# Inverse norms of the local attention heads: logarithm and exponential as seed, one Newton step, clamp on GpSimd

## Chip, cores, metric

The kernel runs on one core of one Trainium2 chip, in one launch, with float32 inputs and outputs. The metric is the device time of one execution in microseconds (us); the time before is the median of three runs. Engines are named as in the profile: PE (TensorE, with PEld for its weight loads), DVE (VectorE), ACT (ScalarE), POOL (GpSimd), SP (the DMA queue of SyncE). L12 is line 12 of the kernel before.

## What is computed

Four residual layers work on x (4 sequences of 512 tokens, 128 features). The change touches the third layer's second half alone, a local transformer of six blocks (reference cut to that):

```python
def attn_layer(x, Wqkv, qs, ksc, Wo):              # 16 heads of 64
    q, k, v = split_heads(x @ Wqkv)
    q = l2norm(q) * qs                             # t / max(norm(t), 1e-12)
    k = l2norm(k) * ksc
    q = q * cos * scale + rotate_half(q) * sin * scale
    k = k * cos * inv + rotate_half(k) * sin * inv
    out = local_attention(q, k, v)                 # windows of 32, each sees itself and the one before
    return out @ Wo
for i in range(6):
    x = attn_layer(shift_tokens(x), Wqkv[i], q_scale[i], k_scale[i], Wo[i]) + x
    x = ffn_layer(shift_tokens(x), ...) + x        # layer norm, gated gelu of width 341
```

The rotation doesn't change which factor a head is divided by, so the kernel rotates first and multiplies by the inverse norm afterwards.

## The kernel before

**Stages.** A preparation and a first part (two cross attentions, mixture of experts), a middle part, the local transformer (`local_transformer`, L1695), and a last part (cross attention, experts). The first, middle and last part are ordered by a small planner (`Plan`) with costs per engine. The local transformer isn't: it runs under a manual schedule, so that each engine executes its instructions in the order in which the loop from L2033 writes them.

**Tiles and pipeline.** The transformer has 96 tiles: 6 blocks, 4 sequences, 4 tiles of 128 tokens. Iteration n of the loop works on three tiles at once: T (number n) is projected and rotated, T1 (n - 1) gets its scores and softmax, T2 (n - 2) its average over the values and its output projection. Between them a feed-forward row F (one sequence of one block) advances by a quarter: `ff_stage` with phase 0 to 3 over four iterations. Four iterations are called a round below.

**The steps of a tile**, with the lines that the prediction uses:
- `queries_or_keys`: a product of y with 512 columns of the weights into a bank ps_mm (L1779, PE), and its square (L1781, ACT). Four of these per tile: q and k, two groups of eight heads each.
- `rotate`: on DVE the product with the cosine table (L1789), with the swapped sine table (L1792), and the sum of the squares per head (L1801, into ss); on POOL the sum of the two products (L1802).
- `normalise`, after the fourth rotation: clamp and scale of ss to -ss/2 (L1812, DVE), a bit-trick seed of 1/sqrt(ss) (L1813, DVE), three Newton steps of four operations each (L1817 to L1820, POOL), all on 128x32; then four products of the rotated heads with the inverse norms (L1823, POOL, 128x512).
- `turned`, an iteration later: transposes of the heads on PE (L582, helper `to_features`), copies to qT and kT on ACT (L1835), and for kT a copy of 32 columns of the tile before on POOL (L1831).
- `scores` on PE (L1879 the mask, L1888 the products) into the bank pair ps_sc; `softmax`: maximum and difference on DVE (L1898, L1899), exponential on ACT (L1904).
- `probabilities`: transposes of P on PE (L582) and copies on ACT (L1909); `average` on PE (L1919); `normalised` on DVE (L1928, L1929); `attended` copies on ACT (L1938); `project_out` on PE (L1943); `residual` on DVE (L1950).
- `values`: two products on PE (L1858), copied by ACT (L1859), then shifted by DMAs from SP.
- The feed-forward row: `ff_gate` (L1978, gelu L1981 on ACT), `ff_up` (L1989), `ff_down` (L2001), its layer norm with DVE's L522. These use ps_sc as well.

Transposes, value products and so on share two PSUM banks (ps_tr), and ps_sc is one pair of banks, so a reader that is late holds the next PE group back.

At the end of an iteration the order is: `rotate(T, 1, 1)`, `normalise(T)`, `softmax(T1)`, `project_out(T2)`, `residual(T2)`, `values(T)`. On DVE, L1812 and L1813 thus stand between the last rotation and the maximum L1898. On ACT, between the aT copies L1938 and the exponential L1904 there is nothing, in some iterations the copy of `swap` and a table load. In five iterations (the last of each block but the final one) `tables` puts six products on POOL ahead of the rotations' sums (L1760, L1766).

ACT's function tables are loaded where an instruction needs another set: in each feed-forward row once ahead of the gelu in phase 1 and once ahead of the first exponential after the gelu of phase 2.

Of the kernel before, what the change touches and what calls it, by code (L numbers as in the profile page):

```python
# [22 lines left out]
I32 = mybir.dt.int32  # L23
U32 = mybir.dt.uint32
AF = mybir.ActivationFunctionType
ALU = mybir.AluOpType
# [12 lines left out]
MASKED = -1e30  # L39
CAP0 = max(1, math.ceil(math.ceil(NTT * 128 * 2 * 1.25) / E))  # L40
CAP3 = int(round(2 * NTT * 128 * 1.05 / E))
NOWHERE = 1e6
ROW = D + 2
CH_W = [128, 128, DI - 256]
# [77 lines left out]
def bc(ap, shape, *axes):  # L122

    for a in axes:
        ap = ap.unsqueeze(a)
    return ap.to_broadcast(shape)
# [112 lines left out]
def tile_kernel(ctx: ExitStack, tc: tile.TileContext, A: dict, out: bass.AP):  # L239
    nc = tc.nc  # L240
    V, G, SC, PE, DMA = nc.vector, nc.gpsimd, nc.scalar, nc.tensor, nc.sync
# [21 lines left out]
    @contextmanager  # L263
    def planned():

        plan = Plan(engines, new_bank)
        yield plan
        with banks(), tc.manual_schedule():
            plan.run()
# [15 lines left out]
    def p_tr(*shape):  # L285
        return psum(shape, "tr", 2)
# [54 lines left out]
    for b in range(B):  # L341
        t = xpool.tile([128, NT, D], F32, name=f"x{b}", tag=f"x{b}")
# [26 lines left out]
    with banks(), tc.tile_pool(name="prep", bufs=1) as prep:  # L369
# [26 lines left out]
        t = p_tr(128, B, SK)  # L396
# [3 lines left out]
        t = p_tr(128, 4, D)  # L400
# [3 lines left out]
        t = p_tr(128, 8)  # L404
# [3 lines left out]
        t = p_tr(128, 2, E)  # L408
# [59 lines left out]
    def col(r):  # L468
        return cols[:, r : r + 1]
# [6 lines left out]
    sent, back = [], []  # L476
    for i, cap in enumerate((CAP0, CAP3, CAP3)):
        n = -(-E * cap // 128)
# [4 lines left out]
    def clear(pool, i):  # L483
# [5 lines left out]
        def fill(e):  # L489
            e.memset(t, 0.0)  # L490
            e.memset(t[:, 1, D + 1 :], NOWHERE)

# [362 lines left out]
    class Routing:  # L855
# [27 lines left out]
        def row(self, plan, b, after):  # L883
# [88 lines left out]
            def places(e):  # L972
                t = bank.view(128, nk, NT, E)
                for k in range(2):
                    j = k if self.apart else 0
                    if j == k:
                        c = rp.tile(full, F32, name="pl")
                        e.tensor_tensor(c, t[:, j], bc(self.limit[:, j], full, 1), ALU.is_ge)
                        e.scalar_tensor_tensor(
                            c, c, NOWHERE, t[:, j], ALU.mult, ALU.subtract if j else ALU.add  # L980
                        )
# [645 lines left out]
    def last_part():  # L1627

        with ExitStack() as es:
# [4 lines left out]
            b2 = yp.tile([128, E, D], BF16, name="b2")  # L1634
            R = Routing(mp, wr[:, 1], CAP3, True)
            with tc.tile_pool(name="xw3", bufs=2) as wp, planned() as plan:
# [18 lines left out]
            with tc.tile_pool(name="m3w", bufs=2) as wp, planned() as plan:  # L1655
# [21 lines left out]
                def down(e, e0, t, h):  # L1677
# [5 lines left out]
                sends, issued = experts(  # L1683
                    plan, wp, sent[1:], back[1], CAP3, [], None, hidden, down, R.issued,
                    (R.all1, None),
# [9 lines left out]
    def local_transformer(Y):  # L1695
        with ExitStack() as es:
# [8 lines left out]
            def pair(tag):  # L1705

                t = homes["pair"].tile([128, 2, 512], F32, tag=tag, bufs=1, name=f"ps_{tag}")
                return t
# [96 lines left out]
            def normalise(T):  # L1805


                n = 2 * LH
                ss = T.ss.rearrange("p a b -> p (a b)")
                y = small.tile([128, n], F32, name="rn_y")  # L1810
                t = small.tile([128, n], F32, name="rn_t")
                V.tensor_scalar(ss, ss, 1e-24, -0.5, ALU.max, ALU.mult)  # L1812
                V.tensor_scalar(  # L1813
                    y.bitcast(I32), ss.bitcast(I32), -0.5, 0x5F3759DF - 0x40400000, ALU.mult, ALU.add
                )
                for _ in range(3):
                    G.tensor_tensor(t, y, y, ALU.mult)  # L1817
                    G.tensor_tensor(t, t, ss, ALU.mult)
                    G.tensor_scalar(t, t, 1.5, None, ALU.add)
                    G.tensor_tensor(y, y, t, ALU.mult)  # L1820
                for (kind, c), a in sorted(T.rot.items()):
                    o = LH * kind + 8 * c
                    G.tensor_tensor(a, a, bc(y[:, o : o + 8], [128, 8, LD], 2), ALU.mult)  # L1823
# [129 lines left out]
            def ff_moments(F):  # L1953
                F.t = pair("sc")[:, 0].rearrange("p (a b) -> p a b", b=128)
                for tt in range(NT):
                    PE.transpose(F.t[:, tt], Y[F.b][:, 128 * tt : 128 * tt + 128], ident)
                F.xn = lnp.tile([128, NT, D], F32, name="xn")
                SC.copy(F.xn, F.t)
                F.found = moments(F.xn)
# [14 lines left out]
            def ff_gate(F, *chunks):  # L1974
                t = pair("sc")
                for j, c in enumerate(chunks):
                    n, o = CH_W[c], DI + 128 * c
                    PE.matmul(t[:n, j], F.w1[:, o : o + n], F.xnT, start=True, stop=True)  # L1978
                for j, c in enumerate(chunks):
                    n = CH_W[c]  # L1980
                    SC.activation(  # L1981
                        F.h[:n, c], t[:n, j], AF.Gelu, bias=col(R_B1 + (3 + c) * DEPTH + F.i)[:n]
                    )
# [20 lines left out]
            def swap(b):  # L2004

                t = tp.tile([128, S], F32, name="yw")
                SC.copy(
                    t.rearrange("p (t x d) -> p t x d", t=NT, x=2)[:, :, ::-1],
                    Y[b][:, 0:S].rearrange("p (t x d) -> p t x d", t=NT, x=2),
                )  # L2010
                swapped[b] = t

            def ff_stage(F, phase, second):
                F.w1, F.w2 = loaded[F.i][3:5]
                if phase == 0 and not second:
                    ff_moments(F)
                elif phase == 1:
                    ff_gate(F, 0, 1) if second else ff_turn(F)
                elif phase == 2 and second:
                    ff_up(F, 0, 1)  # L2020
                elif phase == 2:
                    ff_gate(F, 2)
                elif phase == 3:
                    ff_down(F) if second else ff_up(F, 2)

# [4 lines left out]
            loaded = {0: load(0)}  # L2030
            tabs = {0: tables(loaded[0][5])}
            swap(0)
            for n in range(len(tiles) + 10):  # L2033
                T = tiles[n] if n < len(tiles) else None
                T1 = tiles[n - 1] if 0 <= n - 1 < len(tiles) else None
                T2 = tiles[n - 2] if 0 <= n - 2 < len(tiles) else None
                m, phase = divmod(n - 6, 4)
                F = rows[m] if 0 <= m < len(rows) else None
                if T:
                    if n % 16 == 7 and T.i + 1 < DEPTH:  # L2040
                        loaded[T.i + 1] = load(T.i + 1)
                    if n == 4:
                        fill, send, send_back = clear(lnp, 1)
                        fill(G)
                        send(DMA)
                        send_back(DMA)
                    if n % 16 == 15 and T.i + 1 < DEPTH:
                        tabs[T.i + 1] = tables(loaded[T.i + 1][5])
                    T.before = tiles[n - 1] if T.tt else None
                    T.w, T.wv, T.wo = loaded[T.i][:3]  # L2050
                    T.tabs = tabs[T.i]
                    queries_or_keys(T, 0, 0)
                if T2:
                    probabilities(T2)
                if T:
                    queries_or_keys(T, 0, 1)
                    rotate(T, 0, 0)
                if F:
                    ff_stage(F, phase, False)
                if T2:  # L2060
                    average(T2, 0)
                if T1:
                    turned(T1, 0)
                if T:
                    queries_or_keys(T, 1, 0)
                if T2:
                    normalised(T2, 0)
                if T:
                    rotate(T, 0, 1)
                if T2:  # L2070
                    average(T2, 1)
                if T1:
                    turned(T1, 1)
                if T:
                    queries_or_keys(T, 1, 1)
                if T2:
                    normalised(T2, 1)
                if T:
                    rotate(T, 1, 0)
                if T2:  # L2080
                    attended(T2)
                if T and T.tt == NT - 1 and n + 1 < len(tiles):
                    swap(tiles[n + 1].b)
                if T1:
                    scores(T1)
                if T:
                    rotate(T, 1, 1)
                if T:
                    normalise(T)
                if T1:  # L2090
                    softmax(T1)
                if T2:
                    project_out(T2)
                    residual(T2)
                if F and phase == 0:
                    ff_norm(F)
                if T:
                    values(T, 0)
                    values(T, 1)
                if F:  # L2100
                    ff_stage(F, phase, True)

            for b in range(B):
                for r, o in ((slice(0, 64), 0), (slice(64, 128), 1)):
                    t = p_tr(128, NT, 64)
# [6 lines left out]
    with tc.tile_pool(name="y", bufs=1) as yp:  # L2112
        Y = []
        for b in range(B):
            y = yp.tile([128, S + 1], F32, name=f"y{b}", tag=f"y{b}")
# [29 lines left out]
```

## Time and profile before

| what | value |
|---|---|
| median of 3 runs | 2536.09 us (2535.72 to 2539.29) |
| profiled execution | 2544.82 us, its span 2543.0 us |
| granted PE clock, mean of the span | 0.944 |
| local transformer (first scores to last scores) | 564.3 to 2207.9 us |
| one tile there, mean | 17.3 us |
| L1812, mean | 833 ns; L1813: 182 ns |
| one Newton step on POOL | 240 + 253 + 297 + 253 ns |
| L1802 / L1823, mean | 1275 / 1044 ns |
| table load on ACT | 1283 ns |

Lines of the profile read: line, engine, operation, output <- inputs, shapes, count; then busy time in us, mean ns of one, and the idle time ahead of it with what ended it. A timeline row has the start in us, the duration, engine, line, and in brackets the idle time of the engine and its releaser. A row of the waits has total us, number of times, and the longest.

### The profile page before, as it was taken

To read this page: it belongs to the slowest core of one execution; us is meant where nothing else is said; L and a number is where in the kernel's file an instruction comes from. 1 tells how busy PE (TensorE), PEld (TensorE's weight loads), DVE (VectorE), ACT (ScalarE), POOL (GpSimd) and SP (SyncE) were. 2 spreads that over 40 slices of the span, in tenths; PEclk is the share of its full clock that TensorE was granted. 3 is DMA by queue.
4 is the path that set the end of the run, shared out by engine and by line. 5 is a ranking of instruction groups with operands and counts; after the bars stand their busy time and mean duration, and the time that the engine had idled before them with its cause. 6 is when DMAs were issued, how large, how long until landed. Compare 5 with 4: busy or idle time off the path is not lost.

```text
span 2543.0 us, 87670 instructions
## 1 busy us (share of the span) xinstructions
PE 2287.4 (90%) x37341; PEld 1489.2 (59%) x37341; DVE 1789.3 (70%) x4010; ACT 1245.4 (49%) x2186; POOL 1549.6 (61%) x2620
## 2 busy tenths in 40 slices
PE   7959879968999999999999999999999999878676
PEld 3537744536666666666666666666666666634465
DVE  5436355757888888888888888788888888646422
ACT  3523234535555555555555555555555555514232
POOL 2241232447777777777777777777777777532333
PEclk9868989979999999999999999999999999969788
DMA  6201110015311121111211121111211111102023
GB/s 160 82 20 40 37 41 2 1 49 110 105 28 34 33 61 43 32 28 34 75 28 34 34 71 34 32 28 47 60 29 34 33 27 34 28 27 58 19 70 85
DMA packets 134305, 116.21 MB, mean 46 GB/s; under 512 B 29505, under 2 KB 102700, under 8 KB 133916
## 3 DMA queue, kind: packets, MB, share of 16 engines
q1 hardware_dynamic: 128373, 102.81, 15.5%
q0 software_dynamic: 4608, 7.35, 0.9%
q8 instruction: 296, 4.85, 0.8%
q14 instruction: 93, 0.76, 0.1%
q10 hardware_dynamic: 935, 0.43, 0.1%
HBM read 42.84 MB, written 21.52 MB: 25 GB/s over the span
## 4 chain that ended last, share of the span: by engine, by line
PE 54%; DVE 24%; issue 7%; ACT 6%; POOL 4%; DMA 2%; another core or an unknown queue 1%; SPq 1%; ACTq 0%; POOLq 0%; DVEq 0%
PE ps_tr L582 8%; PE ps_mm L1779 8%; DVE rc L1789 4%; DVE rs L1792 4%; DVE ss L1801 4%; PE ps_av L1919 3%; PE ps_av L1943 3%; PE ps_tr L1858 3%; PE ps_sc L1989 3%; PE ps_sc L2001 3%; PE ps_sc L1888 2%; DVE P L1899 2%; PE ps L773 2%; DVE la_mx L1898 2%; PE ps L782 2%
## 5 line engine op out<-in xcount | busy, mean ns | idle before, releaser
L1802 POOL TENSOR_TENSOR rc<-rc,rs 128x512 f32<-128x512 f32 x384 | 488.4, 1275 | 229.3 <-DVE rs L1792 187.6
L1779 PE MATMUL ps_mm<-wqk,y 128*128 128x512 f32 x768 | 397.7, 600 | 11.0 <-DVE rs L1792 7.6
L1823 POOL TENSOR_TENSOR rc<-rc,rn_y 128x512 f32<-128x512 f32 x384 | 388.8, 1044 | 7.5
L1789 DVE TENSOR_TENSOR rc<-ps_mm,tabs 128x512 f32<-128x512 f32 x384 | 262.5, 684 | 163.0 <-ACT sq L1781 147.6
L1904 ACT ACTIVATE P<-P 128x1024 f32<-128x1024 f32 x96 | 101.5, 1057 | 419.8 <-DVE P L1899 419.8
L1781 ACT ACTIVATE sq<-ps_mm 128x512 f32<-128x512 f32 x384 | 231.0, 602 | 150.5 <-PE ps_mm L1779 103.0
L1792 DVE TENSOR_TENSOR rs<-ps_mm,tabs 128x512 f32<-128x512 f32 x384 | 261.6, 681 | 5.8 <-POOL rc L1802 5.7
L1801 DVE TENSOR_REDUCE ss<-sq 128x8 f32<-128x512 f32 x384 | 259.5, 676 | 0.0
L582 PE MATMUL ps_tr<-cst,rc 128*128 128x128 f32 x1536 | 211.4, 281 | 8.7 <-POOL rc L1823 4.5
L1919 PEld LDWEIGHTS ps_av<-v,PT 64*32 64x32 f32 x12288 | 138.0, 105 | 126.7 <-PE ps_tr L582 55.0
L1943 PE MATMUL ps_av<-aT,wo 128*128 128x128 f32 x1536 | 199.0, 282 | 4.5 <-issue 4.4
L1943 PEld LDWEIGHTS ps_av<-aT,wo 128*128 128x128 f32 x1536 | 180.8, 193 | 13.5 <-issue 4.7
L582 PEld LDWEIGHTS ps_tr<-cst,rc 128*128 128x128 f32 x1536 | 165.6, 141 | 28.7 <-POOL rc L1823 5.6
L1919 PE MATMUL ps_av<-v,PT 64*32 64x65 f32 x12288 | 169.1, 225 | 6.4 <-DVE attn L1929 5.9
L1017 POOL DMA_INDIRECT back<-ye,to x80 | 78.0, 975 | 157.5 <-DVE ye L1131 111.9
L1888 PE MATMUL ps_sc<-kT,qT 64*32 64x64 f32 x12288 | 146.4, 225 | 30.0 <-issue 22.6
L1888 PEld LDWEIGHTS ps_sc<-kT,qT 64*32 64x32 f32 x12288 | 139.8, 105 | 40.9 <-issue 27.0
L1779 PEld LDWEIGHTS ps_mm<-wqk,y 128*128 128x128 f32 x768 | 124.9, 193 | 61.0 <-issue 45.0
L763 ACT ACTIVATE P<-ps,deltaT 77x512 f32<-77x512 f32 x192 | 115.4, 683 | 73.6 <-PE ps L757 68.3
L1835 ACT COPY kT<-ps_tr 128x512 f32<-128x512 f32 x192 | 103.3, 589 | 86.1 <-PE ps_tr L582 84.9
L1835 ACT COPY qT<-ps_tr 128x512 f32<-128x512 f32 x192 | 103.2, 589 | 74.8 <-PE ps_tr L582 72.4
L1929 DVE TENSOR_TENSOR attn<-ps_av,la_den 128x512 f32<-128x512 f32 x192 | 132.8, 691 | 6.6
(392 smaller groups left out, 4510.8 us busy)
## 6 DMA issues: line engine op xcount, KB each, us to landing
v<-v SPq DMA_DIRECT2D x432, 65.0 KB
v<-v SPq DMA_DIRECT2D x96, 195.0 KB
wqk<-in_L_ffn_Wqkv_dram SPq DMA_DIRECT2D x24, 256.0 KB
sent<-xn SPq DMA_DIRECT2D x2, 2210.0 KB
xe<-sent SPq DMA_DIRECT2D x16, 260.0 KB
back<-xn SPq DMA_DIRECT2D x2, 2048.0 KB
raw<-in_L_ffn_W_dram SPq DMA_DIRECT2D x8, 512.0 KB
yb<-back SPq DMA_DIRECT2D x16, 256.0 KB
```

Of the source, the lines that this page charges most:

```text
L582: PE.transpose(t[:, i], src[:, i], ident)
L1779: PE.matmul(t, lhs, T.w[2 * kind + c], start=True, stop=True)
L1781: SC.activation(sq, t, AF.Square)
L1789: V.tensor_tensor(a, t, bc(T.tabs[:, 2 * kind, tt], [128, 8, LD], 1), ALU.mult)
L1792: V.tensor_tensor(r.rearrange("p h (x d) -> p h x d", x=2), t.rearrange("p h (x d) -> p h x d", x=2)[:, :, ::-1], bc(T.tabs[:, 2 * kind + ...
L1801: V.tensor_reduce(T.ss[:, kind, 8 * c : 8 * c + 8], sq, AX.X, ALU.add)
L1802: G.tensor_tensor(a, a, r, ALU.add)
L1823: G.tensor_tensor(a, a, bc(y[:, o : o + 8], [128, 8, LD], 2), ALU.mult)
L1835: SC.copy(t[:, 4 * c : 4 * c + 4, lead:], to_features(T.rot[kind, c].rearrange("p (k x) d -> p k (x d)", x=2)),)
L1888: PE.matmul(T.banks[32 * w : 32 * w + 32, z, k], T.qT[r, k, 32 * w : 32 * w + 32], T.kT[r, k, 32 * w : 32 * w + 64], start=False, stop=Tru ...
L1919: PE.matmul(T.means[32 * w : 32 * w + 32, x0, k], T.PT[r, 4 * g + k, 32 * w : 32 * w + 32], (T.v1 if w % 2 else T.v2)[r, x0, 4 * g + k], s ...
L1943: PE.matmul(t, T.wo[:, c], T.aT[:, c], start=(c == 0), stop=(c == 7))
```

## The change

`normalise` is rewritten, and ACT's tables are loaded by hand at two places. The clamp and scale move from DVE to POOL. The seed is exp(-0.5 ln(ss)), two ACTIVATE instructions on ACT, which must come from one table set that holds both functions. One Newton step on POOL stays of three; the four products stay. The load of the set with logarithm and exponential is written at the start of the transformer's loop and, in each feed-forward row, right after the gelu of phase 2. In the order of the built program no other table loads are in the transformer than these and the gelu's.

```diff
+EXP_LN = "natural_log_exp_and_others"
...
                 ss = T.ss.rearrange("p a b -> p (a b)")
                 y = small.tile([128, n], F32, name="rn_y")
                 t = small.tile([128, n], F32, name="rn_t")
-                V.tensor_scalar(ss, ss, 1e-24, -0.5, ALU.max, ALU.mult)
-                V.tensor_scalar(
-                    y.bitcast(I32), ss.bitcast(I32), -0.5, 0x5F3759DF - 0x40400000, ALU.mult, ALU.add
-                )
-                for _ in range(3):
-                    G.tensor_tensor(t, y, y, ALU.mult)
-                    G.tensor_tensor(t, t, ss, ALU.mult)
-                    G.tensor_scalar(t, t, 1.5, None, ALU.add)
-                    G.tensor_tensor(y, y, t, ALU.mult)
+                G.tensor_scalar(ss, ss, 1e-24, -0.5, ALU.max, ALU.mult)
+                SC.activation(y, ss, AF.Ln, scale=-2.0)
+                SC.activation(y, y, AF.Exp, scale=-0.5)
+                G.tensor_tensor(t, y, y, ALU.mult)
+                G.tensor_tensor(t, t, ss, ALU.mult)
+                G.tensor_scalar(t, t, 1.5, None, ALU.add)
+                G.tensor_tensor(y, y, t, ALU.mult)
                 for (kind, c), a in sorted(T.rot.items()):
                     o = LH * kind + 8 * c
                     G.tensor_tensor(a, a, bc(y[:, o : o + 8], [128, 8, LD], 2), ALU.mult)
...
                 elif phase == 2:
                     ff_gate(F, 2)
+                    SC.preload_act_table_set(EXP_LN)
...
             swap(0)
+            SC.preload_act_table_set(EXP_LN)
             for n in range(len(tiles) + 10):
```

In the changed kernel the line numbers are one larger up to L1812 and one smaller from L1823 on: L1802 becomes L1803, L1823 becomes L1822, L1904 becomes L1903.

## The prediction

> **What bounds the kernel now.** I read the page first (shares), then busy time by stage, then the waits between 600 and 2000 us, then the timeline of one round of four tiles. Page and stage:
>
> ```profile
> PE 2287.4 (90%) x37341; PEld 1489.2 (59%) x37341; DVE 1789.3 (70%) x4010; ACT 1245.4 (49%) x2186; POOL 1549.6 (61%) x2620
> ```
> ```profile
> 560.00:2208.00 1648.00, 1573.64 (x31367) 1055.05 (x31374) 1345.40 (x2468) 937.95 (x1609) 1270.68 (x2221) 1.00 0.17 44
> ```
>
> The second line is the local transformer, the only stage that the change touches: PE busy 1573.6 of 1648 us (95%) at full clock, DVE 82%, POOL 77%, ACT 57%. PE is the bound, so only its gaps can be won. The waits (us in total, times, longest) say who makes gaps:
>
> ```profile
> ACT P L1904 <- DVE P L1899: 354.9, 81, 5.4
> ...
> PEld ps_tr L582 <- ACT v L1859: 33.6, 23, 2.2
> ...
> PE ps_sc L1888 <- POOL kT L1831: 6.1, 5, 1.2
> ```
>
> ACT stands idle 4.4 us per tile for the softmax difference P; PE waits for ACT's copies of the values, which are queued behind P's exponential; and five times PE waits for POOL. One such place in the timeline (start, duration, engine, line):
>
> ```profile
> 1344.29 0.68 DVE L1801 TENSOR_REDUCE ss<-sq 128x8 f32<-128x512 f32 x1
> 1344.52 1.27 POOL L1802 TENSOR_TENSOR rc<-rc,rs 128x512 f32<-128x512 f32 x1 [0.50 <-DVE rs L1792]
> 1345.00 0.82 DVE L1812 TENSOR_SCALAR ss<-ss 128x32 f32<-128x32 f32 x1
> 1345.86 0.18 DVE L1813 TENSOR_SCALAR rn_y<-ss 128x32 int32<-128x32 int32 x1
> 1345.95 1.22 DVE L1898 TENSOR_REDUCE la_mx<-ps_sc 128x16 f32<-128x1024 f32 x1
> ...
> 1347.21 1.23 DVE L1899 TENSOR_TENSOR P<-ps_sc,la_mx 128x1024 f32<-128x1024 f32 x1
> ...
> 1348.46 1.06 ACT L1904 ACTIVATE P<-P 128x1024 f32<-128x1024 f32 x1 [5.01 <-DVE P L1899]
> ...
> 1348.94 1.12 DVE L522 TENSOR_SCALAR xn<-xn,ln_mv,ln_rs 128x128 f32<-128x128 f32 x4
> 1349.43 1.06 ACT L1859 COPY v<-ps_tr 128x512 f32<-128x512 f32 x2
> ...
> 1350.05 1.15 PE L582 MATMUL ps_tr<-cst,P 128*128 128x128 f32 x8 [1.19 <-ACT v L1859]
> 1350.29 1.04 POOL L1823 TENSOR_TENSOR rc<-rc,rn_y 128x512 f32<-128x512 f32 x1
> ```
>
> The scores had ended by 1344.3, yet the maximum L1898 starts at 1345.95, because L1812 and L1813 stand ahead of it on DVE. A tiny L1812 lasts 0.82 us: it ends 0.03 us after POOL's add L1802 (1344.52 + 1.27 = 1345.79). All 96 of them do (753 to 1109 ns). From L1898 the delay runs through L1899, the exponential and the value copies to PE's transposes.
>
> **What the Trainium skill says.** "SBUF — State Buffer", Who interferes with whom: a VectorE tensor_scalar in a 2-port mode and a GpSimd instruction share a port pair, and the later one blocks fully. L1812's end at POOL's end agrees. "ScalarE: Activation LUTs", What ACT_TABLE_LOAD costs: about 1283 ns and a drain of 1380 ns; the trace has 1283 (L1904 and L1981) but no drain, as the gelu after the load at 1296.99 starts at 1298.28. Same page, Table sets: one set holds both ln and exp; nothing in this trace shows ln. Its price of an ACTIVATE without pointers, 186 ns + 0.833 N, gives 612 for L1781, measured 602.
>
> **The change, part by part.** DVE loses L1812 and L1813: from L1801's end (1344.97) to L1898's start is 0.98 us, so the maximum can start about 0.96 us earlier wherever the scores are done, and 0.33 where PE's scores are held up (at 1324.5 they end at 1326.72, L1898 started at 1327.08).
>
> POOL loses two Newton steps (eight operations; step to step 1.36 us in the timeline, so 2.7) and gains the clamp. Not shown in this form; nearest is L1819 at 297 ns, bounds 0.25 (L1818) to 0.5; I take 0.35. ACT gains Ln and Exp on 128x32: the page's price gives an estimate of 0.21 each, upper bound L1781's 0.60; I take 0.25 plus 0.1 for each hand-over. Chain: add ends 1345.79, clamp 1346.2, Ln 1346.5, Exp 1346.9, one Newton step to 1348.4; the products L1823 start near 1348.5 instead of 1350.29.
>
> The new wait: Ln stands on ACT ahead of P's exponential and the value copies. P would be ready at 1344.97 + 2.49 = 1347.5, Exp is done at 1346.9. With both at 0.60 and the clamp at 0.5 it ends at 1347.7, 0.2 late. So the cover is ACT's idle time before L1904, and the price of the Ln and Exp is nothing, or 0.2 us per tile at the far end. POOL's clamp waits only for DVE's L1801, done before POOL's own add ends.
>
> Table loads: the order of the built program has one load for gelu and one for the exponentials per feed-forward row, as before. The latter moves: from the idle slot before L1904 to right after the third gelu, ahead of the qT copies L1835. At 1302.05 that is busy ACT: the copies would go from 1302.19 to about 1303.4. Behind them: the squares, kT copies, attention transposes. But ACT gets there earlier, as exponential, value copies and gelus all follow P. Working that iteration through with P 0.95 and PE 0.5 earlier, durations from the timeline: third gelu 1300.5 to 1301.15, load to 1302.45, qT copies to 1303.5 (without the load 1302.7), the square behind them 1303.75 to 1304.35, where DVE's L1789 wants it at 1305.34 - 0.95 = 1304.39; the kT copies can't start before PE's transposes at 1304.3 anyway. I charge 0.1 us per row; had nothing shifted it would be 0.35 (attention transposes at 1306.3 for 1305.96). One more load stands at the start of the stage, where PE waits 3.3 us for the first wqk, and one goes from the last part (L763): nothing.
>
> What PE gets, from start-to-start distances of consecutive PE groups in the timeline over all 96 tiles, less the distance without a wait (5th percentile); means per round of four tiles, 24 rounds:
> - Transposes of P after the first q product: 0.86 us without a wait, 1.4 to 1.5 lost in half the rounds, 0.3 in those where an issue gap of 1.1 us came just before. Won: 12 x 0.96 + 11 x 0.33 = 15.1.
> - Feed-forward products waiting for P to leave ps_sc: L1978 0.27, L1989 0.33, L2001 0.12; all covered by 0.95. Won: 0.72 x 24 = 17.3.
> - What follows these (third gate product behind ACT's gelus 0.13, refills 0.22): 0.35 x 24 = 8.4.
> - kT copies L1831 in the five iterations that compute tables on POOL: 1.4 lost; POOL is 1.8 earlier, but PE by then 1.0: won 5 x 0.8 = 4.0.
> - The second iteration, where PE waits 4.53 us for L1823: 1.7.
> - Table load: -0.1 x 24 = -2.4.
>
> Sum 44.1. The profiled execution took 2544.8 (span 2543.0), so 2500.7; it lies 8.7 above the median of the runs, 2536.1, and I take the sum from the median: 2492. Not won: issue gaps of about 1.1 us, 27 times (31 us), and PE waiting for attn (0.26 per round), which follow PE itself. Where P's stall goes, next late is DVE's own row of rotations, then PE.
>
> **The rivals.**
> - Table load exposed: ACT has no idle time there, and 1.28 us comes onto every row. For: ACT is continuous from 1296.99 to 1303.3. Against: the working above, PE runs two groups ahead. 24 x 1.28 = 31: 2536 - 44 + 31 = 2523.
> - ACT as the new gate: Ln and Exp end after P. At 0.2 late plus slow hand-overs of another 0.3 half the 0.96 is lost: about 2514. Against: 0.6 us of slack.
> - PE takes it back: gaps reappear elsewhere, in issue gaps or the granted clock. For: 95% busy. Against: the gaps have named releasers on DVE and ACT; clock 1.00. 2536.
> - Slower, by the port: the products L1823 now start near 1348.5, and the layer norm's L522, which ended at 1350.06, 0.2 us before them, falls among them. L522 is a tensor_scalar on SBUF like L1812. If it blocks until all four (4.05 us) are done, DVE starts the next tile some 3.2 us late, less 0.4 of idle time before L1928: 2.8 x 24 = 67, so 2536 - 44 + 67 = 2559. It decides from 1.9 us per row. Against: L522 ran beside POOL's small operations at 342 ns and at 341 with POOL idle (after 2233 us), so it doesn't take the pair.
> - The change undone by loads at each tile (ln and exp from different sets): the built order has none.
>
> **How the numbers follow.** Forecast 0.66 (own range 2482 to 2506: the load at 0 or 0.35, the follow-up terms at nothing or full); load exposed 0.09; ACT gate 0.07; more than summed (below 2480, P's other waits gone too) 0.04; PE takes it back 0.08; port 0.06. Measurement tells 0.2%, 5 us, from no change. Faster 0.66 + 0.09 + 0.07 + 0.04 and a hundredth of the fourth: 0.87; same 0.07; slower 0.06. Leaving out below 2480, the fourth and the port is 0.18: range 2480 to 2523.
>
> **What would show it.** L1898 starting some 0.03 us after L1801; P's exponential still released by DVE, not by Exp; L1859 no more among PE's long waits; L1978 and L1989 without DVE P; kT waits near nothing; products 1.8 us earlier; L522 still at 342 ns; the load between gelu and qT. It is wrong if L1904 starts behind Exp, if L522 grows, or if PE's waits for qT or kT copies grow by 1 us a row.

## The result and the profile after

The kernel before was run once more beside the changed one, so it has four runs here.

| | before | changed |
|---|---|---|
| median of 4 runs | 2537.50 us (2535.72 to 2539.29) | 2496.91 us (2493.47 to 2502.75) |
| profiled execution, its span | 2544.82, 2543.0 us | 2497.58, 2495.8 us |
| granted PE clock, mean of the span | 0.944 | 0.951 |
| first scores to last scores | 1643.6 us | 1608.6 us |

The ratio is 0.9839, interval 0.982 to 0.9858: 40.6 us faster by the medians, where the prediction's sum was 44.1. Of the 47.2 us between the two profiled executions, 35.0 lie between the first and the last scores, 4.5 ahead of the first scores, and 7.6 after the last (335.1 against 327.5). The 35.0 lie in the stage that the change touches. The other two are not put down to it: in the profiled executions of the eight kernels on the next two chips of this document the stretch ahead spreads over 553 to 564 us and the stretch behind over 331 to 339 us. The granted clock was 0.80 behind the last scores before and 0.83 after. On those two chips the kernels with the shorter transformer stage also had the shorter stretch behind it (331 to 333 us against 335 to 339), on the last chip there was no such difference (313 to 314 us), so whether some of it comes with the change stays open.

From the page of the changed kernel: shares of the engines, the engines on the chain that ended last, and two groups (line, operation, count, then busy us, mean ns, and idle time before with its releaser).

```profile
PE 2257.5 (90%) x37341; PEld 1487.1 (60%) x37341; DVE 1746.9 (70%) x3818; ACT 1292.4 (52%) x2379; POOL 1383.5 (55%) x1948
...
PE 72%; DVE 15%; issue 4%; ACT 3%; DMA 2%; POOL 2%; another core or an unknown queue 2%; SPq 1%; POOLq 0%; ACTq 0%; DVEq 0%
...
L1903 ACT ACTIVATE P<-P 128x1024 f32<-128x1024 f32 x96 | 101.5, 1057 | 92.1 <-DVE P L1898 92.1
L1814 ACT ACTIVATE rn_y<-ss 128x32 f32<-128x32 f32 x96 | 22.0, 229 | 238.4 <-POOL ss L1813 238.4
```

PE is now on 72% of the chain (54% before) and DVE on 15% (24% before): the path runs more through the engine that is the bound. ACT's exponential still waits for DVE's P and never for the new Exp, but only 92.1 us in the whole execution (between 600 and 2000 us 76.9, where the prediction shows 354.9). Most of the rest of that idle time now stands ahead of Ln, which waits for POOL's clamp.

The local transformer alone (window, its length, then busy us of PE, PEld, DVE, ACT and POOL):

```profile
560.00:2170.00 1610.00, 1559.41 (x31479) 1061.64 (x31471) 1302.82 (x2277) 982.31 (x1796) 1102.84 (x1550) 1.00 0.17 45
```

PE is busy 96.9% of it (95.5% before) at the same full clock. DVE's busy time fell only from 1345.4 to 1302.8, and its share is 81% against 82%.

PE's waits between 600 and 2000 us, first before, then after (us in total, times, longest):

```profile
PE ps_sc L1888 <- issue: 18.1, 20, 1.3
PE ps_tr L582 <- ACT v L1859: 15.4, 16, 1.4
PE ps_sc L1888 <- POOL kT L1831: 6.1, 5, 1.2
...
PE ps_sc L1989 <- DVE P L1899: 3.9, 14, 0.3
...
PE ps_sc L1978 <- DVE P L1899: 2.0, 9, 0.5
```
```profile
PE ps_sc L1887 <- issue: 23.2, 23, 2.1
...
PE ps_tr L583 <- ACT v L1858: 3.9, 14, 0.3
...
PE ps_sc L1966 <- DVE xn L523: 2.4, 5, 0.6
```

The waits for ACT's value copies fell to a quarter; those for POOL's kT and for DVE's P are gone. Most of what is left has the releaser "issue": the engine waited for nothing that the trace can name. One wait is new: L1966, the transposes of the feed-forward input, for the layer norm L523.

The same place of a round as in the prediction, after the change (start, duration, engine, line, idle time of the engine with its releaser):

```profile
1324.85 0.68 DVE L1802 TENSOR_REDUCE ss<-sq 128x8 f32<-128x512 f32 x1
1325.08 1.27 POOL L1803 TENSOR_TENSOR rc<-rc,rs 128x512 f32<-128x512 f32 x1 [0.50 <-DVE rs L1793]
1325.45 1.22 DVE L1897 TENSOR_REDUCE la_mx<-ps_sc 128x16 f32<-128x1024 f32 x1
1326.43 0.33 POOL L1813 TENSOR_SCALAR ss<-ss 128x32 f32<-128x32 f32 x1
1326.70 1.23 DVE L1898 TENSOR_TENSOR P<-ps_sc,la_mx 128x1024 f32<-128x1024 f32 x1
1326.80 0.23 ACT L1814 ACTIVATE rn_y<-ss 128x32 f32<-128x32 f32 x1 [2.94 <-POOL ss L1813]
1327.06 0.23 ACT L1815 ACTIVATE rn_y<-rn_y 128x32 f32<-128x32 f32 x1
...
1327.95 1.06 ACT L1903 ACTIVATE P<-P 128x1024 f32<-128x1024 f32 x1 [0.67 <-DVE P L1898]
1328.43 3.44 DVE L523 TENSOR_SCALAR xn<-xn,ln_mv,ln_rs 128x128 f32<-128x128 f32 x4
1328.74 4.05 POOL L1822 TENSOR_TENSOR rc<-rc,rn_y 128x512 f32<-128x512 f32 x4
...
1329.54 1.15 PE L583 MATMUL ps_tr<-cst,P 128*128 128x128 f32 x8 [0.28 <-ACT v L1858]
```

The maximum L1897 starts as the last sum of squares ends. Ln and Exp are over at 1327.29, and P's exponential starts 0.66 us later, in all 96 tiles at least that, so the new operations sit in idle time. The products L1822 start 3.66 us after the start of POOL's last add; before it was 5.77 (1350.29 - 1344.52). PE's transposes of P wait 0.28 us instead of 1.19. But the four operations of L523 (the layer norm, L522 before) last 3.44 us, where they took 1.12: they run beside the products now.

### The profile page after: what moved, and what is told of

Read it like the earlier page. It is cut to its first block, busy times and chain, and to the rows that moved or that the text cites. A ratio compares the mean times of both kernels' runs of the same rounds, so it can differ in the third digit from the quotient of the medians.

```text
span 2495.8 us, 86737 instructions
## 1 busy us (share of the span) xinstructions
PE 2257.5 (90%) x37341; PEld 1487.1 (60%) x37341; DVE 1746.9 (70%) x3818; ACT 1292.4 (52%) x2379; POOL 1383.5 (55%) x1948
## 3 DMA queue, kind: packets, MB, share of 16 engines
q1 hardware_dynamic: 128373, 102.81, 15.8%
## 4 chain that ended last, share of the span: by engine, by line
PE 72%; DVE 15%; issue 4%; ACT 3%; DMA 2%; POOL 2%; another core or an unknown queue 2%; SPq 1%; POOLq 0%; ACTq 0%; DVEq 0%
PE ps_tr L583 12%; PE ps_mm L1780 10%; PE ps_av L1942 6%; PE ps_av L1918 5%; PE ps_tr L1857 5%; PE ps_sc L1887 4%; DVE xn L523 3%; PE ps_sc L1977 3%; PE ps_sc L1988 3%; PE ps_sc L2000 2%; PE ps L774 2%; PE ps L1313 2%; PE ps L783 2%; PE ps L1682 2%
## 5 line engine op out<-in xcount | busy, mean ns | idle before, releaser
L1803 POOL TENSOR_TENSOR rc<-rc,rs 128x512 f32<-128x512 f32 x384 | 489.5, 1276 | 385.4 <-DVE rs L1793 329.5
L1822 POOL TENSOR_TENSOR rc<-rc,rn_y 128x512 f32<-128x512 f32 x384 | 388.7, 1044 | 7.5
L1802 DVE TENSOR_REDUCE ss<-sq 128x8 f32<-128x512 f32 x384 | 259.5, 676 | 0.0
L1903 ACT ACTIVATE P<-P 128x1024 f32<-128x1024 f32 x96 | 101.5, 1057 | 92.1 <-DVE P L1898 92.1
L1814 ACT ACTIVATE rn_y<-ss 128x32 f32<-128x32 f32 x96 | 22.0, 229 | 238.4 <-POOL ss L1813 238.4
```

The lines of the kernel that those rows point to most:

```text
L1802: V.tensor_reduce(T.ss[:, kind, 8 * c : 8 * c + 8], sq, AX.X, ALU.add)
L1803: G.tensor_tensor(a, a, r, ALU.add)
```

## The experiments

Each kernel has its interval from five rounds against the kernel before on the same chip. Chips differ: the kernel before took 2545.0 us on that of the first four kernels, 2542.2 on that of the next four, 2489.4 on that of the last three. So the ratios are compared; 0.1% is 2.5 us.

**Three steps again.** The changed kernel with all three Newton steps on POOL: POOL's part of the change undone, DVE's kept.

```diff
+                for _ in range(3):
-                G.tensor_tensor(t, y, y, ALU.mult)
...
+                    G.tensor_tensor(t, y, y, ALU.mult)
...
```

> Changed kernel, but with all three Newton steps kept on GpSimd (POOL 2.7 us longer per tile than in the changed kernel, and about as long as before); VectorE stays relieved of clamp and seed. Theory (the gain is VectorE's, in front of the maximum of the scores): nearly the whole gain stays, 2497 to 2512; the table iterations lose their 4 us again, PE may wait some 0.3 us for the later products, and the layer norm no longer meets them, which gives something back. Rival (the gain is POOL's shorter chain): back to 2525 to 2540.

Measured 2515.8 us, ratio 0.9878 (0.9846 to 0.9911): DVE's part alone brings some 31 of the 41 us. Against 0.9839 two steps on POOL cost some 10 us. The intervals touch, but the kernel with the moved load below, on the same chip and otherwise the changed one, has all its runs at 2503.8 to 2508.9, these lie at 2514.3 to 2520.3. The layer norm ran at 348 ns in the median here, as the products came after it. PE's waits (600 to 2200 us) show what the steps cost in turn:

```profile
PE ps_sc L1888 <- POOL kT L1831: 12.4, 5, 2.5
...
PE ps_tr L583 <- POOL rc L1823: 4.5, 16, 0.3
```

Five waits for kT of up to 2.5 us, in the iterations in which POOL also makes tables, and 16 small waits of the transposes for the products. So later products and an undisturbed layer norm go together, and the first costs more.

**One step, old seed.** The kernel before with one Newton step: POOL's part alone (one step behind this seed gives less exact inverse norms).

```diff
-                for _ in range(3):
+                for _ in range(1):
```

> Kernel before with one Newton step instead of three; clamp and bit-trick seed stay on VectorE. It leaves out two Newton steps, so that the inverse norms are coarser. Theory: VectorE is as late as before, so no gain but kT copies and start (-7 us), and the products now fall into the layer norm at 1347.6 instead of 1350.3, which costs up to 22 us: 2528 to 2555. Rival (POOL's shorter chain is the gain): 2500 to 2515.

Measured 2555.67 us, ratio 1.0036 (1.0018 to 1.0055): slower than the kernel before, with nothing but work taken away. Its layer norm lasted 833 ns in the mean, so the earlier products meet it. Whether the meeting is what makes it slower is tested further below.

**The load in ACT's idle slot.** The changed kernel with the second table load where ACT waits anyway, ahead of `normalise`.

```diff
                     ff_gate(F, 2)
-                    SC.preload_act_table_set(EXP_LN)
...
+                if F and phase == 2:
+                    SC.preload_act_table_set(EXP_LN)
                 if T:
                     normalise(T)
```

> Changed kernel with the load of the logarithm and exponential set moved from right after the third gelu to the idle time of ACT ahead of the logarithm. Theory (the load was hidden, 0.1 us per row): 2491 to 2498. Rival (the load lies open): 2466 to 2475.

Measured 2507.39 us, ratio 0.9835 (0.9807 to 0.9863), no different from 0.9839. The load after the gelu cost nothing that can be measured. By the two intervals that is told to some 9 us: it rules out the 31 us of the exposed load, not the 2.4 us of the prediction.

**The clamp on DVE.** The changed kernel with the clamp where it was.

```diff
-                G.tensor_scalar(ss, ss, 1e-24, -0.5, ALU.max, ALU.mult)
+                V.tensor_scalar(ss, ss, 1e-24, -0.5, ALU.max, ALU.mult)
```

> Changed kernel with the clamp back on VectorE; logarithm, exponential and the single Newton step as changed. Theory (the clamp's wait for POOL's addition, 0.8 of the 0.96 us, was what delayed the maximum): most of the gain is gone, 2522 to 2535, and the clamp again ends with POOL's addition. Rival (POOL's chain or the seed is the gain): 2497 to 2508.

Measured 2550.04 us, ratio 1.0018 (0.9998 to 1.0038): one instruction moved back takes all 40 us. That is more than was expected. The clamp lasts 825 ns in the mean again, and the layer norm 962; both hold DVE in the same kernel.

**The changed kernel again**, on the chip of the next three.

> The changed kernel again, as the reference of this set. All theories: ratio to the kernel before 0.982 to 0.986.

2501.56 us, ratio 0.9837 (0.9807 to 0.9867).

**The layer norm on ACT.** The changed kernel with the four operations of L523 as ACTIVATE (scale 1/std, offset -mean/std from two small operations on POOL), issued ahead of `normalise`: nothing of DVE is left for the products to meet there.

```diff
+                mv, rs = F.found
+                F.off = small.tile([128, NT], F32, name="ln_off")
+                G.tensor_tensor(F.off, mv[:, :, 0], rs, ALU.mult)
+                G.tensor_scalar(F.off, F.off, -1.0, None, ALU.mult)
...
-                layernorm(F.xn, F.xn, F.found)
+                for t in range(NT):
+                    SC.activation(
+                        F.xn[:, t], F.xn[:, t], AF.Identity,
+                        scale=F.found[1][:, t : t + 1], bias=F.off[:, t : t + 1],
+                    )
...
+                if F and phase == 0:
+                    ff_norm(F)
                 if T:
                     normalise(T)
...
-                if F and phase == 0:
-                    ff_norm(F)
```

> Changed kernel, with the feed-forward layer norm's four tensor_scalar taken from VectorE to ACT (Identity with scale and bias, in ACT's idle time ahead of the logarithm; two small operations more on POOL). So nothing on VectorE can meet POOL's products. If the meeting (3.4 instead of 1.1 us per round in the changed kernel's trace) costs PE time: the row of iterations around it falls from 15.6 to about 15.2 us, 8 to 12 us in all, ratio 0.979 to 0.981. If it is hidden in VectorE's idle time, as the kernel with three steps suggests: ratio 0.982 to 0.986.

Measured 2488.03 us, ratio 0.9792 (0.9763 to 0.982), the lowest ratio of all. Its six runs lie at 2478.5 to 2493.1, those of the changed kernel beside it at 2495.8 to 2512.3. Its transformer stage:

```profile
560.00:2160.00 1600.00, 1554.46 (x31511) 1062.02 (x31511) 1227.67 (x2189) 1016.50 (x1889) 1104.95 (x1586) 1.00 0.18 45
```

PE is busy 97.2% there, DVE 77% instead of 81%. So removing the meeting brings 0.45%, 11 to 12 us by the ratios (13.5 between the medians on this chip). But four DVE operations per round went as well; whether they alone bring something is asked below.

**ACT held.** The changed kernel with eight more Exp of 128x32 behind the seed's, into a tile that nobody reads: some 2 us more on ACT ahead of P's exponential.

```diff
                 SC.activation(y, y, AF.Exp, scale=-0.5)
+                more = small.tile([128, n], F32, name="rn_more")
+                for _ in range(8):
+                    SC.activation(more, ss, AF.Exp)
```

> Changed kernel with eight more exponentials of 128x32 into a scratch tile behind the one of the seed, so that ACT is held about 2 us longer in each tile and the softmax's exponential starts about when it did in the kernel before, while VectorE and POOL stay as changed. Theory (about half the gain passes through the exponential and the value copies, the other half through VectorE leaving ps_sc earlier): 20 to 30 us are lost, ratio 0.992 to 0.996. If all passes through ACT: ratio 1.00. If ACT's part is nothing: 0.984.

Measured 2524.32 us, ratio 0.9944 (0.9925 to 0.9963). This is how the rival "ACT as the new gate" looks (waits between 600 and 2200 us):

```profile
PE ps_tr L583 <- ACT v L1861: 26.0, 23, 1.5
...
PE ps_sc L1980 <- ACT fh L1983: 13.3, 21, 1.9
...
ACT P L1906 <- DVE P L1901: 2.6, 3, 2.2
```

P's exponential no longer waits for DVE (2.6 us in all), and PE waits for the value copies (26.0 us) and gelus (13.3) behind it. In the changed kernel, in the same window, the exponential waits for DVE 89.2 us, and PE waits 4.5 us for the value copies and 1.0 for a gelu.

**The old seed behind P.** The kernel before with the clamp on POOL and its bit-trick seed on DVE behind the softmax difference, three steps: DVE's relief without Ln, Exp or a shorter chain.

```diff
...
-                V.tensor_scalar(ss, ss, 1e-24, -0.5, ALU.max, ALU.mult)
+                G.tensor_scalar(ss, ss, 1e-24, -0.5, ALU.max, ALU.mult)
+                if T1:
+                    softmax(T1)
                 V.tensor_scalar(
                     y.bitcast(I32), ss.bitcast(I32), -0.5, 0x5F3759DF - 0x40400000, ALU.mult, ALU.add
...
```

> Kernel before, all three Newton steps and the bit-trick seed kept, but the clamp on POOL and the seed on VectorE behind the softmax difference L1899 instead of ahead of the maximum L1898; ACT does nothing new. Theory (the place ahead of the maximum was the cost): a good part of the gain without logarithm and exponential, less what PE now waits for products that come 1.5 us later: ratio 0.988 to 0.995. If the seed on ACT is itself the gain: ratio 1.000 or above.

Measured 2538.79 us, ratio 0.9982 (0.9969 to 0.9996). The expectation failed: relief for DVE that is paid for with later products is worth almost nothing. PE's waits (600 to 2200 us) say why:

```profile
PE ps_tr L582 <- POOL rc L1825: 23.7, 50, 0.8
...
PE ps_sc L1890 <- POOL kT L1833: 12.4, 5, 2.5
```

The seed comes behind two operations of 1.22 and 1.23 us, three steps follow, and PE waits 50 times for the products. What the change adds to DVE's relief is a seed on ACT, which doesn't stand behind DVE's softmax: with it and three steps PE waited 16 times for the products (4.5 us), and the ratio was 0.9878.

**The layer norm on ACT, three more kernels.** The edit of the layer norm above on the kernel before; on the kernel before with one step; and on the changed kernel with the clamp on DVE. The first asks whether that edit is worth anything where nothing meets.

> Kernel before with the layer norm's four tensor_scalar on ACT. In the kernel before they met no product of POOL. Theory (what the same edit gave on the changed kernel, about 12 us, was the meeting): here next to nothing, ratio 0.998 to 1.001. If it was VectorE's 1.1 us themselves: ratio 0.994 to 0.996.

Measured 2491.29 us, ratio 1.0009 (0.9999 to 1.0018): nothing. So in the changed kernel its gain most likely is the meeting.

> Kernel before with the layer norm on ACT and one Newton step instead of three (two steps left out, coarser inverse norms); clamp and seed on VectorE. Shows what POOL's shorter chain is worth by itself, without the meeting. Theory: kT copies and start, 6 us or so: ratio 0.996 to 0.999. If the slowness of one step with the old seed (1.0036) was not the meeting: above 1.001.

Measured 2480.62 us, ratio 0.9963 (0.9949 to 0.9976). With the layer norm out of the way two steps fewer do bring time, 0.46% or some 12 us against the kernel just above; with it in the way they cost 0.36%. So the meeting turns a gain into a loss.

> Changed kernel with the layer norm on ACT, but the clamp on VectorE: differs from the kernel of ratio 0.979 in the clamp's engine alone. Theory (clamp ending with POOL's addition is what holds the maximum up): 0.994 to 0.999. If the clamp on VectorE was slow only through the meeting: 0.981 to 0.985.

Measured 2465.28 us, ratio 0.9902 (0.9888 to 0.9916), between what the theories had given. The one instruction in question, on DVE here and on POOL in the kernel with the layer norm on ACT (duration lowest/median/highest in ns, first and last start):

```profile
L1813 DVE TENSOR_SCALAR ss<-ss x96: 753/822/1111, 516.3 to 2135.3; 128x32 f32<-128x32 f32 x96
```
```profile
L1813 POOL TENSOR_SCALAR ss<-ss x96: 329/329/354, 543.2 to 2132.0; 128x32 f32<-128x32 f32 x96
```

Here too the clamp is 822 ns on DVE and 329 on POOL. It is not ACT's seed that comes later with the clamp on DVE: there the clamp ends 0.04 us after POOL's last add, on POOL some 0.4 us after it. Without the meeting the parts of the change can be put side by side in this order, each a difference of two ratios times 2537 us:

| part | ratios | us |
|---|---|---|
| two Newton steps fewer | 1.0009 to 0.9963 | -12 |
| seed from DVE to ACT (with the loads) | 0.9963 to 0.9902 | -15 |
| clamp from DVE to POOL | 0.9902 to 0.9792 | -28 |
| products meet the layer norm | 0.9792 to 0.9837 | +11 |

The sum follows from the first ratio and the last, so it checks nothing. Each row is uncertain by some 4 to 11 us, and the third crosses two chips. The transformer stage alone, first scores to last scores in the profiled execution of each, agrees for the first three rows: 1647.7, 1639.0, 1623.8 and 1592.4 us, so -9, -15 and -31. In another order the parts come out differently: with DVE relieved and nothing meeting, two steps fewer are worth some 22 us (0.9878 to 0.9792, across two chips).

## Why the prediction was right, and where it failed

**Right: the mechanism.** What mattered was not that DVE worked less but what stood ahead of the maximum. DVE's share of the stage hardly moved, yet PE's gaps behind it closed. The clamp is the heavy part (28 us), and it is heavy only on DVE: it held DVE in every kernel that left it there (824 to 836 ns in the mean) and took 329 ns on POOL, where 0.35 us had been assumed. Its end at POOL's end, less than 0.05 us behind it in all 96 tiles, is what the Trainium skill ("SBUF — State Buffer", Who interferes with whom) describes; the move and its undoing show its price in this kernel.

**Right: ACT's cover.** Two groups between 560 and 2170 us show what ACT paid:

```profile
L2022 ACT ACT_TABLE_LOAD x23 | 29.5, 1283 | 0.4
...
L1815 ACT ACTIVATE rn_y<-rn_y 128x32 f32<-128x32 f32 x95 | 21.8, 229 | 3.0
```

Ln and Exp took 229 ns each, where 0.25 had been taken. They end 0.66 us ahead of P, where the working had 0.6. With 2 us more on ACT that cover is gone and the kernel loses 1.1%. The rivals "load exposed" and "ACT as the new gate" fell by these two experiments. Of "PE takes it back" the traces show at most 6 us, in issue gaps that also differ between executions. The granted clock didn't bring the gain: on the chip where the changed kernel ran again its median was 0.948 for both kernels.

**The terms of the sum.** PE's intervals, start to start of consecutive groups, less the distance without a wait (the lower 5th percentile of the two kernels), measured in both profiled executions:

| term | predicted, us | in the traces |
|---|---|---|
| transposes of P behind the value copies | 15.1 | 25.1 to 8.7: 16.4 |
| feed-forward products waiting for P | 17.3 | 15.8 to 0.0: 15.8 |
| what follows these | 8.4 | 7.9 to 0.3: 7.6 |
| kT copies in five iterations | 4.0 | 7.0 |
| second iteration, PE behind L1823 | 1.7 | 1.8, but 0.8 more for kT there |
| table load | -2.4 | not seen (experiment, to some 9 us) |
| issue gaps | 0 | -6 |
| what follows L1966, which waits for the layer norm | 0 | -8.5 |

The first three came out within 1.5 us each. The kT term was mis-sized: of 1.4 us lost in each of the five iterations 0.8 was to be won, as PE was to come 1.0 us earlier itself, and all 1.4 went. POOL's products were 2.1 us earlier where 1.8 had been worked out; the rest of the difference no run explains. The intervals between the first and the last scores sum to 114.3 us lost before and 79.8 after. That is 34.5 won, and the stage is 35.0 us shorter. So the stage gained less than the 44.1 of the sum: what the prediction counted on came in full, but two terms that it had at nothing took time back, the layer norm 8.5 us and, in these two executions, the issue gaps 6. The 40.6 us between the medians are nearer to the forecast than the 35.0 that these traces place in the stage.

**Wrong: "so it doesn't take the pair".** The step in the port rival argued that L522 does not share the port with POOL, because it ran at 342 ns beside POOL's small operations. Beside the products it does wait for POOL. The prediction had named "if L522 grows" as a sign of being wrong, and it grew. The layer norm after and before (lowest/median/highest ns):

```profile
L523 DVE TENSOR_SCALAR xn<-xn,ln_mv,ln_rs x96: 341/1080/1180, 648.6 to 2193.2; 128x128 f32<-128x128 f32 x96
```
```profile
L522 DVE TENSOR_SCALAR xn<-xn,ln_mv,ln_rs x96: 332/342/348, 655.3 to 2233.9; 128x128 f32<-128x128 f32 x96
```

In the median it takes 1080 ns, about the length of one product L1822 (1044), and in the timeline four of each run in step. PE pays for it at the transposes of the layer norm's output: the group behind them started 0.53 us after their start in all 23 rows before, and 0.59 to 1.34 us after it now. With three steps and with the layer norm on ACT it is 0.53 again in every row. The same place before, then after:

```profile
1351.89 0.60 PE L1967 MATMUL ps_sc<-cst,xn 128*128 128x128 f32 x4
1352.42 0.86 PE L1919 MATMUL ps_av<-v,PT 64*32 64x65 f32 x64
```
```profile
1331.38 0.88 PE L1966 MATMUL ps_sc<-cst,xn 128*128 128x128 f32 x4
...
1332.19 1.02 PE L1918 MATMUL ps_av<-v,PT 64*32 64x65 f32 x64
```

The evidence was too weak, as the prediction looked at L522's own duration alone. The trace before has a sign of the meeting on POOL's side. A Newton operation away from the layer norm, and the same line beside it:

```profile
1348.16 0.29 POOL L1819 TENSOR_SCALAR rn_t<-rn_t 128x32 f32<-128x32 f32 x1
...
1349.52 0.35 POOL L1819 TENSOR_SCALAR rn_t<-rn_t 128x32 f32<-128x32 f32 x1
```

In all 23 rows the L1819 beside L522 lasts 351 to 367 ns, and the other 265 in the trace last 289 to 307. There it was POOL that was held, and by 0.06 us. The runs show the waiting; that the port is the reason is not shown by them.

The rival was priced too high as well: it let DVE wait until all four products were done, 2.8 us per round. DVE got in after each product instead; it lost 2.3 us per round, most of it in time that PE didn't miss, and the whole came to 8.5 us in the intervals and 11 to 12 by the ratios, not 67. That the sum still came out near is partly luck: the table load (2.4), of which nothing was seen, and the larger kT term (3.0) made up for half of it. On the kernel before with one step, the same meeting decides the sign (1.0036 with it, 0.9963 without).

**Open.** The issue gaps of PE have no releaser in the trace. They cost 31 us before and 35 after (at one more place 3 and 5), and in the changed kernel's other profiled execution 43, so no part of the 40 us is put down to them. They were longest in the kernels with the ratios 1.0036 (one step, old seed: 50 us) and 1.0018 (clamp on DVE: 47). So the traces don't name what PE waited for in a large part of those two losses. Nor was it settled why the clamp on DVE costs 45 us with the meeting (0.9839 to 1.0018) and 28 without: two delays on one queue in the same iteration may add up to more than each alone, but no run here shows it. And the layer norm's edit removes both its lengthening and its own 1.1 us per round from DVE; on the kernel before the second was worth nothing, on the changed kernel it wasn't tried apart.

## What to carry to other kernels

On an engine that runs in order, look at what stands directly ahead of the instruction that others wait for: a tiny operation whose duration is far above its size, and which ends when another engine's operation ends, is likely to be waiting inside its own bar, where no list of waits shows it. When a chain is shortened, ask what the longer operations behind it will now run beside. To see whether two operations disturb each other, compare the durations of both with and without the other, and try it with operations of the size that will meet: at one length the wait may be small and on the other engine. The parts of a change need not add up: here POOL's part alone made the kernel 0.36% slower, DVE's part alone brought some 31 us, and both together 41. So an experiment that adds or undoes one part tells its worth beside the others that are there, not its worth as such.

## What the hardware showed beyond this

- A tensor_scalar of DVE with two per-partition operands (128x128, float32, 342 ns) was stretched to 1080 ns beside a queue of 128x512 tensor_tensor operations on POOL, one POOL operation at a time, not until the queue was empty. Beside the small operations of the Newton steps it kept 342 ns, and one of those, a tensor_scalar of 292 ns, lasted 353.
- Neither of the two table loads per row, 1283 ns each, showed a drain around it: ACT's idle time was some 17 ns before each and 11 to 12 ns behind it in the median, and moving one of them changed the ratio by 0.0004 (told to some 0.0034).
- A kernel with less work on POOL was slower (1.0036), and one instruction per tile, 0.33 us on POOL in place of 0.82 on DVE, decided 1.1 to 1.8% of the time.
